# First-block attention scores on 64x64 tiles over 192 queries in every group, and a chunk's raw sums on two column tiles

## The chip, the cores and the metric

The kernel runs on one core of a Trainium2 chip. A core has TensorE (matrix products, PE in the profile, with its weight loads as PEld), VectorE (DVE), ScalarE (ACT), GpSimd (POOL) and SyncE (SP), which here only issues transfers. The engines run side by side, each working through its own queue in order, and wait for each other through semaphores. All share the on-chip memory SBUF; TensorE writes to PSUM, eight banks of 128 partitions with 512 f32 numbers each. Transfers (DMA) run beside the engines, but the instruction that issues one takes time on the queue of the engine that issues it.

The metric is device time in microseconds (us). Before the change the median of three runs is 3545.7 us (3537.46 to 3548.12).

## The reference

The input x is 32 sequences of 256 tokens with 256 channels. A conditioned state-space layer comes first, then two layers of windowed attention and a gated feed-forward, and x is added at the end. Cut to what matters here:

```
xr, gate = split(x @ W_in.T);  xr = xr + cond          # 512 channels each
xc = silu(causal_conv4(xr) + b);  xn = layernorm(xc)
Bm, Cm, dt = split(xn @ W_xproj.T)                     # 16 states each: 48 sums
dt = tanh(dt @ W_dt.T + b_dt) * 0.01
Ad = 1 - dt * tanh(A_log);  Bd = Bm * min(|xn|, 1)
for t:  h = clip(h * Ad[t] + Bd[t] xn[t], -10, 10);  y[t] = Cm[t] . h
cond_out = ((y + D * xn) * silu(gate)) @ W_out.T

for each of 2 layers:
    q, k, v = split(shift(x) @ wqkv)                   # 8 heads of 64
    q, k = rotary(l2norm(q)), rotary(l2norm(k))        # scale 8 on q
    sim[i, j] = q_i . k_j   where  0 <= i - j <= 128,  otherwise masked
    x = x + (softmax(sim) @ v) @ wo
    x = x + (a * gelu(g)) @ w2,   a, g = split(layernorm(shift(x)) @ w1)
out = x_input + x
```

With 256 tokens and windows of 128 there are two blocks of keys. The first block (keys 0 to 127) is seen by all 256 queries, with a mask: key j only by queries j to j + 128. So keys 0 to 63 are seen by queries 0 to 191 at most, and keys 64 to 127 by queries 64 to 255. The second block is seen by queries 128 to 255 only.

## The kernel before

The 32 sequences are four groups of eight (`GB`). For each group the state-space layer is a scan over 256 steps (`group_scan`). It works in chunks of 32 steps (`CH`), so there are eight chunks a group and 32 in all. The states of one step fill 128 partitions (16 states by 8 sequences) with 512 channels; one VectorE instruction (`step`, L722) makes the step. It needs the normalised row of that step, repeated over the states by a transfer (`load_rows`, xrep) and scaled by ScalarE (`scale_row`, L712) two steps ahead. The agenda of the scan is a list of step numbers: `at(s, what)` puts work at step s.

What a chunk needs of figures is made ahead of its first step s0. `raw_sums` (at s0 - 27, L520) multiplies the convolved channels xc of the chunk, 4 blocks of 128 channels by 256 columns (8 sequences by 32 steps), with the 48 columns of W_xproj, widened to 64 with zeros. The sums stand in 64 partitions of a PSUM bank. `raw_copy` (s0 - 25, L528) has ScalarE copy them to SBUF, and `raw_turn` (s0 - 24, L535) issues three transfers on ScalarE's queue, one for each of Bm, Cm and dt, that turn them so that states and sequences lie on 128 partitions and steps on the free axis (`rw`). `figures_in` (s0 - 7, L636) reads rw.

Beside the scan runs the attention and feed-forward of the groups that are done. There are 64 calls of attention (4 groups by 2 layers by 8 sequences), each in eight stages. `scores` (L1232) makes the scores transposed, keys on partitions and queries on the free axis, in parts of one key block and two or four heads with even and odd heads (r = 0, 1) in two PSUM banks, one for each 64 rows of the head dimension. Stage 2 has the first key block of heads 0 to 3 and the whole second block, stage 3 the first block of the others. `exponentials` (L1244) makes exp of both banks.

The mask of the first key block is made in two ways. In group 0 (`apart` is false) a product of an identity and `mask_t` (bf16, L1205) first writes the mask into the whole bank, and the scores are added to it; they come in square pieces of 64 keys by 192 queries, on four quarters of the TensorE array (rows by r, columns by half of the keys). In groups 1 to 3 (`apart`) the scores are written plainly, 128 keys by 256 queries, on two row tiles, and after exp VectorE multiplies by `mask_1`, which is 0 or 1 (L1260). The second block is always one piece of 128 keys by 128 queries on two row tiles, and GpSimd zeroes what is masked (L1255).

All PSUM tiles share the same eight banks (`ps_w`), so TensorE waits when no bank has been freed. The program text is written as one list: scan steps are placed between stages by `scan_to`, and a planner orders the instructions of each engine at compile time, except those that are kept in program order.

Of the kernel before, what the change touches and what calls it, by code (L numbers as in the profile page):

```python
# [10 lines left out]
FP = mybir.dt.float32  # L11
# [8 lines left out]
P = 128  # L20
S = 256
# [3 lines left out]
NC_ = DI // P  # L25
NS = 16
GB = 8
CH = 32
# [9 lines left out]
DH = 64  # L38
W = 128
# [34 lines left out]
def kernel(  # L74
# [29 lines left out]
    nc = tc.nc  # L104
# [58 lines left out]
    for j in range(NJ):  # L163
# [16 lines left out]
    ident_b = const.tile([P, P], BF, tag="ident_b", name="ident_b")  # L180
# [3 lines left out]
        out=mask_t[:, 0:W], in_=mask_t[:, 0:W], compare_op=ALU.is_ge, fill=MASKED_LOW,  # L184
# [3 lines left out]
        out=mask_t[:, W : 2 * W], in_=mask_t[:, W : 2 * W], compare_op=ALU.is_ge,  # L188
# [14 lines left out]
    wx_sb = const.tile([P, NC_, 4 * NS], FP, tag="wx_sb", name="wx_sb")  # L203
# [15 lines left out]
    for i in range(2):  # L219
        t = const.tile([P, NI * (P + GB)], FP, tag=f"ly{i}", name=f"ly{i}")  # L220
# [3 lines left out]
    def program(ctx, exact):  # L224
        rpool = ctx.enter_context(tc.tile_pool(name="res", bufs=1, reuse_waits="tile"))
        wpool = ctx.enter_context(tc.tile_pool(name="weights", bufs=1, reuse_waits="tile"))
        sp = ctx.enter_context(tc.tile_pool(name="sp", bufs=1, reuse_waits="tile"))
# [6 lines left out]
        ps_w = ctx.enter_context(tc.tile_pool(name="psw", bufs=8, space=PSUM, reuse_waits="tile"))  # L234

        def bank(pool, tag, name):
            return pool.tile([P, DI], FP, tag=tag, name=name)
# [141 lines left out]
        def group_scan(g):  # L379
# [12 lines left out]
            ck = [{} for _ in range(NCH)]  # L392
# [122 lines left out]


            def raw_sums(c):
                pr = bank(ps_w, "w", "ps_raw")
                for ch in range(NC_):
                    nc.tensor.matmul(  # L520
                        pr[0 : 4 * NS, 0 : GB * CH], wx_sb[:, ch, :], ck[c]["xc"][:, ch],
                        start=(ch == 0), stop=(ch == NC_ - 1),
                    )
                ck[c]["pr"] = pr

            def raw_copy(c):
                raw = sp.tile([4 * NS, GB * CH], FP, tag="raw", name="raw")
                nc.scalar.copy(raw, ck[c].pop("pr")[0 : 4 * NS, 0 : GB * CH])  # L528
                ck[c]["raw"] = raw

            def raw_turn(c):
                rw = sm.tile([P, 3, CH], FP, tag="rw", name="rw")
                raw = ck[c].pop("raw")
                for i in range(3):
                    nc.scalar.dma_start(  # L535
                        out=rw[:, i],
                        in_=raw[i * NS : (i + 1) * NS].rearrange("n (b t) -> n b t", b=GB),
                    )
                ck[c]["rw"] = rw


# [320 lines left out]
            for c in range(NCH):  # L862
# [14 lines left out]
                for ch, s in enumerate((13, 16, 17, 18)):  # L877
                    at(s0 + s + 2, gate_th, c, ch)
                    if not alone:
                        at(s0 + s + 4, gate_out, c, ch)  # L880
                at(s0 - 25, raw_copy, c)
                at(s0 - 24, raw_turn, c)
                for j in range(NJ):
                    s = s0 - 26 + 4 * j
# [45 lines left out]
            if alone:  # L930
                n = (NG - 1) * NCH * 2
# [130 lines left out]
        if exact:  # L1062
# [4 lines left out]
                out=mask[:, 0:W], in_=mask[:, 0:W], compare_op=ALU.is_ge, fill=MASKED,  # L1067
# [3 lines left out]
                out=mask[:, W : 2 * W], in_=mask[:, W : 2 * W], compare_op=ALU.is_ge, fill=MASKED,  # L1071
# [95 lines left out]
        class Attention:  # L1167
# [51 lines left out]
            def products(self, b, kw, i0, n, banks):  # L1219
                qT, kT, _ = self.qkv[b]  # L1220
                nq = S - kw * W
                masked = kw == 0 and not self.apart
                nm = 2 if masked else 1
                mk = W // nm
                for i in range(n):
                    for r in range(2):
                        rows = slice(r * DH, (r + 1) * DH)
                        for m in range(nm):

                            k0 = m * mk  # L1230
                            q0, q1 = (k0, k0 + W + mk) if masked else (0, nq)
                            nc.tensor.matmul(  # L1232
                                banks[r][k0 : k0 + mk, i, q0:q1],
                                kT[rows, i0 + i, kw * W + k0 : kw * W + k0 + mk],
                                qT[rows, i0 + i, kw * W + q0 : kw * W + q1],
                                start=not masked,
                                stop=not masked or i == n - 1,
                            )
# [328 lines left out]
        for t in range(max(stages) + 1):  # L1567
# [3 lines left out]
            g, r = divmod(t + 1 + group - reload, group)  # L1571
# [124 lines left out]
```

## Time and profile before

| | |
|---|---|
| median of three runs | 3545.7 us |
| the profiled execution | 3535.63 us |
| its span, first to last instruction | 3533.5 us |
| TensorE busy | 3418.2 us |
| ps_raw, L520, 128*64 128x256 f32 | 256 instructions, mean 394 ns |
| rw transfers issued on ScalarE's queue, L535 | 96, median 620 ns |
| sc, L1232, 64*64 64x192 f32 (group 0) | 512 instructions, mean 335 ns |
| sc, L1232, 64*128 64x256 f32 (groups 1 to 3) | 768 instructions, mean 402 ns |
| sc, L1232, 64*128 64x128 f32 (second block) | 1024 instructions, mean 275 ns |

In these rows 64*128 is the part of the array that a product uses (contracted rows by output columns), and 64x256 the moving operand. The mean of one instruction is its latency; products follow each other much closer than that, since they are pipelined, and on different tiles of the array they run side by side. What a run of products costs is therefore read from the timeline, from its first start to the start of what follows. Every f32 product stands as two instructions, one bf16 product as one.

The timeline has start in us, duration in us, engine, line, operation, output and inputs, shape, count, and in brackets the idle time before with what ended it. The stretches have for each engine its busy time and its number of instructions, then granted clock, share of the DMA engines, and GB/s. ACTq is the queue of ScalarE, where transfers are issued. A group row has its busy time and the mean of one instruction.

### The profile page before, as it was taken

Reading aid. Unit: us, or ns where it says so; the run is one execution under the profiler, and the core shown is the slowest. Engines: PE = TensorE matmul, PEld = TensorE weight load, DVE = VectorE, ACT = ScalarE, POOL = GpSimd, SP = SyncE. Lnnn points to the kernel's source line nnn. Section 1 sums busy time; section 2 is a strip of 40 time slices with the busy share of each in tenths; the row PEclk is TensorE's granted clock in tenths of the full one; section 3 lists DMA queues with packets and bytes.
Section 4 is the critical chain, followed back from the end, with each engine's and each line's share of the span. In section 5 each row is a group of like instructions: output and inputs, shape, how many; then the busy total and the mean of one; then the engine's idle time right before and its main releaser. Section 6 shows DMA issues by size and latency. Waiting matters only on the chain.

```text
span 3533.5 us, 56484 instructions
## 1 busy us (share of the span) xinstructions
PE 3418.2 (97%) x19580; PEld 2257.4 (64%) x19580; DVE 2683.2 (76%) x5177; ACT 2035.4 (58%) x3663; POOL 1625.6 (46%) x1587
## 2 busy tenths in 40 slices
PE   7999989999999999999999999999999999999999
PEld 4545335666666666666666666666666777777777
DVE  5888898878788788888888888888787655555563
ACT  4666656656666665666666656666566444444442
POOL 4433456544455555544455555544444434333441
PEclk9999999999999999999999999999999999999999
DMA  7787655545454555444454555544444212011111
GB/s 208 215 217 218 198 169 153 136 113 142 129 143 130 150 147 151 136 114 134 117 142 128 148 148 147 137 120 130 118 142 118 61 37 62 13 31 36 37 28 38
DMA packets 487195, 436.65 MB, mean 124 GB/s; under 512 B 247155, under 2 KB 326516, under 8 KB 486772
## 3 DMA queue, kind: packets, MB, share of 16 engines
q1 hardware_dynamic: 401426, 420.41, 42.2%
q10 hardware_dynamic: 85474, 12.53, 2.1%
q8 instruction: 157, 2.57, 0.3%
q14 instruction: 138, 1.13, 0.1%
HBM read 384.06 MB, written 47.19 MB: 122 GB/s over the span
## 4 chain that ended last, share of the span: by engine, by line
PE 63%; DVE 17%; DMA 7%; POOL 5%; ACT 4%; issue 3%; SPq 1%; ACTq 0%; DVEq 0%; POOLq 0%
PE ps_qkv L996 13%; PE pa L1405 13%; DVE h L722 7%; PE po_f L1432 6%; PE y L734 5%; PE ps_wo L1052 4%; PE ov L1289 3%; DMA xrep<-xnd 3%; PE ps_out L814 3%; PE ps_in L401 3%; PE sc L1232 3%; PE tr_qk L1041 2%; PE rs L1269 2%; PE ps_raw L520 2%; DVE acc L491 1%
## 5 line engine op out<-in xcount | busy, mean ns | idle before, releaser
L722 DVE CUSTOM_DVE_ANT_0 h<-h,xrep,lim 128x512 f32<-128x512 f32 x1024 | 917.2, 896 | 137.3 <-ACT xrep L712 93.4
L712 ACT ACTIVATE xrep<-xrep,beta 128x512 f32<-128x512 f32 x960 | 671.6, 719 | 265.5 <-DMA xrep<-xnd 178.2
L996 PE MATMUL ps_qkv<-qkv,res 128*128 128x512 f32 x1536 | 716.0, 601 | 26.6 <-DVE ag L1423 12.5
L1405 PE MATMUL pa<-hT,w 128*128 128x256 f32 (+1 forms) x2816 | 674.7, 382 | 5.1 <-DVE zT L805 5.1
L1405 PEld LDWEIGHTS pa<-hT,w 128*128 128x128 f32 (+1 forms) x2816 | 517.4, 188 | 145.4 <-issue 41.8
L1020 POOL TENSOR_TENSOR rot<-rot,swp 128x512 f32<-128x512 f32 x256 | 345.1, 1348 | 496.7 <-DVE swp L1017 465.9
L996 PEld LDWEIGHTS ps_qkv<-qkv,res 128*128 128x128 f32 x1536 | 282.0, 191 | 311.5 <-issue 247.0
L1026 POOL TENSOR_TENSOR rn<-ss,neg_half 128x8 f32<-128x8 f32 x256 | 457.6, 1788 | 0.0
L734 PE MATMUL y<-h,ly 128*32 128x512 f32 x2048 | 341.1, 606 | 15.7 <-DVE h L722 13.6
L1432 PE MATMUL po_f<-ag,w 128*128 128x256 f32 x1280 | 306.7, 387 | 3.8 <-DVE fo L1443 3.1
L1423 DVE SCALAR_TENSOR_TENSOR ag<-pa,b_sb,ag 128x256 f32<-128x256 f32 x320 | 151.5, 474 | 208.7 <-ACT ag L1416 208.7
L1009 ACT ACTIVATE sq<-ps_qkv,tiny 128x512 f32<-128x512 f32 x256 | 173.3, 685 | 186.3 <-PE ps_qkv L996 129.3
L1432 PEld LDWEIGHTS po_f<-ag,w 128*128 128x128 f32 x1280 | 235.3, 190 | 68.3 <-DVE pT L1260 12.9
L1416 ACT ACTIVATE ag<-pa,b_sb 128x256 f32<-128x256 f32 x320 | 150.0, 469 | 209.7 <-PE pa L1405 206.8
L1357 POOL TENSOR_TENSOR rstd<-ve,neg_half 128x2 f32<-128x2 f32 x64 | 46.5, 726 | 484.9 <-DVE ve L1355 484.8
L1052 PE MATMUL ps_wo<-oT,wo 128*128 128x256 f32 x1024 | 231.6, 379 | 0.0
L1012 DVE TENSOR_TENSOR rot<-ps_qkv,rc_sb 128x512 f32<-128x512 f32 x256 | 175.1, 684 | 71.8 <-ACT sq L1009 70.1
L491 DVE SCALAR_TENSOR_TENSOR acc<-xr,wc_sb,acc 128x256 f32<-128x256 f32 x384 | 183.1, 499 | 50.8 <-POOL acc L480 50.0
L1017 DVE TENSOR_TENSOR swp<-ps_qkv,rs_sb 128x256 f32<-128x256 f32 x512 | 191.8, 416 | 27.6 <-POOL rot L1020 27.5
L1052 PEld LDWEIGHTS ps_wo<-oT,wo 128*128 128x128 f32 x1024 | 194.5, 190 | 27.2 <-ACT th_g L774 0.8
L1032 DVE SCALAR_TENSOR_TENSOR rot<-rn,rot 128x512 f32<-128x512 f32 x256 | 205.7, 841 | 7.5 <-POOL rn L1026 7.5
L1244 ACT ACTIVATE pT<-sc 128x512 f32<-128x512 f32 x384 | 201.6, 601 | 8.2 <-PE sc L1232 6.1
(161 smaller groups left out, 5375.6 us busy)
## 6 DMA issues: line engine op xcount, KB each, us to landing
xrep<-xnd SPq DMA_DIRECT2D x960, 256.0 KB
rb<-inv SPq DMA_DIRECT2D x128, 256.0 KB
xnd<-xn SPq DMA_DIRECT2D x64, 256.0 KB
qkv<-in_wqkv_dram SPq DMA_DIRECT2D x24, 512.0 KB
ahead<-xs_a SPq DMA_DIRECT2D x48, 256.0 KB
xp<-ahead SPq DMA_DIRECT2D x48, 256.0 KB
xd<-xnd SPq DMA_DIRECT2D x192, 64.0 KB
w<-in_w_dram SPq DMA_DIRECT2D x80, 128.0 KB
```

The source lines that it names most:

```text
L491: nc.vector.scalar_tensor_tensor(acc, xr[:, :, k : k + CH], wc_sb[:, ch, k : k + 1], acc, ALU.mult, ALU.add,)
L712: scaled = nc.scalar.activation(bx, ck[c].pop(("bx", t), bx), AF.Copy, scale=ck[c]["beta"][:, t : t + 1])
L722: nc.vector._custom_dve(TENSOR_ADD_SAT, out=h_new, in0=state["h"], in1=bx, s0=ck[c]["lim"][:, 0, t : t + 1], s1=ck[c]["lim"][:, 1, t : t + 1],
L734: nc.tensor.matmul(ck[c]["y", hb][32 * q : 32 * q + 32, :], ly[hb % 2][:, 32 * t : 32 * t + 32], ck[c].pop(("h", hb * TB + t)), start=(i = ...
L996: nc.tensor.matmul(ps, res[b][:, k, t0 : t0 + W], wt["qkv", a][:, k], start=(k == 0), stop=(k == KM - 1),)
L1020: nc.gpsimd.tensor_add(rot, rot, swp)
L1026: nc.gpsimd.tensor_tensor(rn, ss, neg_half, ALU.pow)
L1032: nc.vector.scalar_tensor_tensor(rot, bc(rn, 2, DH), 1e12, rot, ALU.min, ALU.mult)
L1052: nc.tensor.matmul(po[:, d], wt["wo", 0][:, c, d * P : (d + 1) * P], oT[:, c, :], start=(c == 0), stop=(c == NC_ - 1),)
L1244: nc.scalar.activation(p, banks[r], AF.Exp)
L1405: nc.tensor.matmul(dst[x], wt["w1", m][:, k, x], self.h[:, k], start=(k == 0), stop=(k == KM - 1),)
L1432: nc.tensor.matmul(self.po[:, d], wt["w2", 0][:, m, d * P : (d + 1) * P], self.ag[m], start=(m == 0), stop=(m == len(MCH) - 1),)
```

## The change

Raw sums: each of the four products of a chunk becomes two, for the first and the last 16 steps of all sequences, on column tiles 0 to 63 and 64 to 127 of the array. They write to partitions 0 to 63 and 64 to 127 of the same 128 columns of a bank. ScalarE's copy is then 128 partitions by 128, and six transfers of half the size bring it to the same `rw`.

Scores: every part is made in square pieces of 64 keys. In the first key block the pieces span 192 queries in all groups. In groups 1 to 3, where nothing is written beforehand, the 64 queries that a piece leaves out get zeros from one bf16 product for each tile of the array and part (an identity's off-diagonal block, which is zero, times columns of the identity), for all heads of the part at once. Their exp is 1, and the multiplication by `mask_1` makes them 0 as before. The second key block is two pieces of 64 keys by 128 queries.

```diff
--- before.py
+++ after.py
@@ -515,27 +515,34 @@
 
 
             def raw_sums(c):
-                pr = bank(ps_w, "w", "ps_raw")
+                pr = bank(ps_w, "w", "ps_raw")[:, 0 : GB * CH // 2]
+                halves = ck[c]["xc"].rearrange("p c (b h t) -> p c b h t", b=GB, h=2)
                 for ch in range(NC_):
-                    nc.tensor.matmul(
-                        pr[0 : 4 * NS, 0 : GB * CH], wx_sb[:, ch, :], ck[c]["xc"][:, ch],
-                        start=(ch == 0), stop=(ch == NC_ - 1),
-                    )
+                    for h in range(2):
+                        nc.tensor.matmul(
+                            pr[64 * h : 64 * h + 64],
+                            wx_sb[:, ch, :],
+                            halves[:, ch, :, h],
+                            start=(ch == 0),
+                            stop=(ch == NC_ - 1),
+                        )
                 ck[c]["pr"] = pr
 
             def raw_copy(c):
-                raw = sp.tile([4 * NS, GB * CH], FP, tag="raw", name="raw")
-                nc.scalar.copy(raw, ck[c].pop("pr")[0 : 4 * NS, 0 : GB * CH])
+                raw = sp.tile([P, GB * CH // 2], FP, tag="raw", name="raw")
+                nc.scalar.copy(raw, ck[c].pop("pr"))
                 ck[c]["raw"] = raw
 
             def raw_turn(c):
                 rw = sm.tile([P, 3, CH], FP, tag="rw", name="rw")
                 raw = ck[c].pop("raw")
-                for i in range(3):
-                    nc.scalar.dma_start(
-                        out=rw[:, i],
-                        in_=raw[i * NS : (i + 1) * NS].rearrange("n (b t) -> n b t", b=GB),
-                    )
+                for h in range(2):
+                    for i in range(3):
+                        r = 64 * h + i * NS
+                        nc.scalar.dma_start(
+                            out=rw[:, i, h * CH // 2 : (h + 1) * CH // 2],
+                            in_=raw[r : r + NS].rearrange("n (b t) -> n b t", b=GB),
+                        )
                 ck[c]["rw"] = rw
 
 
@@ -1220,15 +1227,23 @@
                 qT, kT, _ = self.qkv[b]
                 nq = S - kw * W
                 masked = kw == 0 and not self.apart
-                nm = 2 if masked else 1
-                mk = W // nm
+                mk = W // 2
                 for i in range(n):
                     for r in range(2):
                         rows = slice(r * DH, (r + 1) * DH)
-                        for m in range(nm):
+                        for m in range(2):
 
                             k0 = m * mk
-                            q0, q1 = (k0, k0 + W + mk) if masked else (0, nq)
+                            if kw == 0 and not masked and i == 0:
+                                qc = (S - mk) * (1 - m)
+                                nc.tensor.matmul(
+                                    banks[r][k0 : k0 + mk, :, qc : qc + mk],
+                                    ident_b[rows, (1 - r) * DH : (2 - r) * DH],
+                                    ident_b[rows, 0 : n * mk],
+                                    start=True,
+                                    stop=True,
+                                )
+                            q0, q1 = (0, nq) if kw else (k0, k0 + W + mk)
                             nc.tensor.matmul(
                                 banks[r][k0 : k0 + mk, i, q0:q1],
                                 kT[rows, i0 + i, kw * W + k0 : kw * W + k0 + mk],
```

## The prediction

> **What bounds the kernel now.** I read the page's busy shares first, then the chain, then the stretches.
>
> ```profile
> span 3533.5 us, 56484 instructions
> PE 3418.2 (97%) x19580; PEld 2257.4 (64%) x19580; DVE 2683.2 (76%) x5177; ACT 2035.4 (58%) x3663; POOL 1625.6 (46%) x1587
> PE 63%; DVE 17%; DMA 7%; POOL 5%; ACT 4%; issue 3%; SPq 1%; ACTq 0%; DVEq 0%; POOLq 0%
> ```
> ```profile
> core 0: us, PE busy (x) PEld busy (x) DVE busy (x) ACT busy (x) POOL busy (x), PEclk, DMA share, GB/s
> 0.00:500.00 500.00, 445.62 (x1847) 230.16 (x1848) 411.83 (x758) 296.18 (x545) 211.36 (x306) 0.95 0.76 209
> 500.00:2600.00 2100.00, 2047.03 (x12277) 1357.03 (x12276) 1734.90 (x3397) 1313.15 (x2389) 1072.68 (x1012) 1.00 0.49 135
> 2600.00:3400.00 800.00, 800.00 (x4717) 571.01 (x4716) 480.53 (x907) 382.96 (x654) 310.49 (x245) 1.00 0.20 54
> ```
>
> TensorE is the bound. From 500 to 2600 us, where the recurrent scan runs beside attention, it is idle 53 of 2100 us, 2.5%. After 2600 us it is never idle. Only before 500 us (TensorE 89%) does VectorE's chain of steps set a good part of the pace. A busy share can hide slack, so the parts are costed by starts: from the first instruction of a run to the start of the next one on TensorE.
>
> ```profile
> 503.19 0.59 PE L1205 MATMUL sc<-mask_t,ident_b 128*128 128x512 bf16 x2
> 503.71 1.97 PE L1232 MATMUL sc<-qT,kT 64*64 64x192 f32 x32
> 505.62 1.06 PE L734 MATMUL y<-h,ly 128*32 128x512 f32 x6
> ...
> 507.14 0.88 PE L1232 MATMUL sc<-qT,kT 64*64 64x192 f32 x16
> 507.95 2.41 PE L996 MATMUL ps_qkv<-qkv,res 128*128 128x512 f32 x5
> ```
> ```profile
> 2018.32 2.02 PE L1232 MATMUL sc<-qT,kT 64*128 64x256 f32 x24
> 2020.27 2.42 PE L1432 MATMUL po_f<-ag,w 128*128 128x256 f32 x10
> ...
> 2023.50 1.13 PE L1232 MATMUL sc<-qT,kT 64*128 64x256 f32 x8
> 2024.56 1.98 PE L996 MATMUL ps_qkv<-qkv,res 128*128 128x512 f32 x4
> ```
> ```profile
> 2051.31 1.52 PE L1289 MATMUL ov<-pT,v_sb 128*64 128x256 f32 x16 [0.28 <-DVE ag L1423]
> 2052.76 0.64 PE L734 MATMUL y<-h,ly 128*32 128x512 f32 x4
> ```
> ```profile
> 2477.26 1.94 PE L520 MATMUL ps_raw<-xc,wx_sb 128*64 128x256 f32 x8
> 2479.13 0.66 PE L550 MATMUL tp_x<-ident,xc 128*128 128x128 f32 x4
> ...
> 2479.63 1.93 ACTq L535 DMA_DIRECT2D rw<-raw  x3
> ...
> 2481.67 0.72 ACT L712 ACTIVATE xrep<-xrep,beta 128x512 f32<-128x512 f32 x1 [1.44 <-DVE h L722]
> 2485.09 0.29 ACT L574 ACTIVATE stat<-nm,stat 128x1 f32<-128x1 f32 x1 [2.70 <-POOL stat L567]
> ```
>
> An f32 product is two instructions in these rows (two passes). The first two fences are the same work in two forms: group 0 (four square tiles, 192 queries) and a later group (two row tiles, 256 queries). A first-block part of two heads takes 507.95 - 507.14 = 0.81 us in the square form and 2024.56 - 2023.50 = 1.06 in the other. With the second key block behind it, the run takes 505.62 - 503.71 = 1.91 and 2020.27 - 2018.32 = 1.95.
>
> **Raw sums, TensorE.** Now eight passes of 256 columns follow each other: 2479.13 - 2477.26 = 1.87 us, that is 8 x 0.216 and 0.14 of entry and exit. (The chain gives 3.43 us for eight passes of 512 columns at L996: 0.43 each, 0.84 ns a column, 0.216 for 256.) Afterwards there are sixteen passes of 128 columns on two column tiles. The values line already runs in that form: its sixteen passes are four pairs of 256 columns and four of 128 and take 2052.76 - 2051.31 = 1.45; less 4 x 0.216 and 0.14 this leaves 0.45, or 0.11 for a pair of 128. So 8 x 0.109 + 0.14 = 1.01, and 0.86 us less for each of 32 chunks. The moving operand becomes runs of 16 elements at a stride of 32; no matmul of the trace shows such a pattern, so the gain lies between 0 (the stride costs what the split saves) and 0.86. I take 0.86: the nearest row, the mask product at L1205 whose moving operand is a repeated pattern and not one run, takes 0.26 us for 512 bf16 columns and shows no penalty. 22 chunks lie after 500 us: 18.9 us. Ten lie in the stage that TensorE only half bounds: half of 8.6, 4.3 us. Together 23.
>
> The values row shows that the two column tiles load their weights beside running products. [...]
>
> **Raw sums, ScalarE and transfers.** The copy goes from 64x256 (363 ns) to 128x128. A 128x32 activation takes 318, so it saves 0 to 0.05 us; I take 0.03. The three issues of rw become six, at a median of 620 ns (552 to 1394) each on ScalarE's queue: 1.86 us more a chunk, net 1.83 x 32 = 58.6 us of ScalarE's time. Queued behind them are the scaling of the scan's rows (L712), which VectorE's step (L722) waits for, then L574 and L581, and copies that free PSUM banks for TensorE. The last fence shows the cover: after the burst ScalarE scales one row and then sits 2.70 us until GpSimd has delivered. 1.83 fits, and rows are scaled two steps ahead of use. In early chunks the idle time comes later. Bounds 0 and 58.6 us; I take 5, near the lower end, because of that gap. The transfers move the same bytes in 64-byte runs; figures_in, which reads them, is due 17 steps after the issue, at least 17 x 0.9 = 15 us (a step, L722, takes 896 ns), against 3.7 us of issuing. SP's and GpSimd's queues are not touched.
>
> **First key block, groups 1 to 3 (48 calls, 96 parts).** 1.06 becomes 0.81 plus the four zero fills of a part (64x128, bf16). Two mask products take 503.71 - 503.19 = 0.52 us: 0.26 for 512 columns, 0.065 for 128. If the four tiles fill side by side the price is 0.065; hidden under other loads it is 0; one after another it is 0.26, the whole gain; worse is a rival below. I take 0.065, since everything else on the four tiles runs side by side. Gain 0.25 - 0.065 = 0.185, x 96 = 17.8 us.
>
> **Second key block, all 64 calls.** Now 1.95 - 1.06 = 0.89 for eight steps of 0.111, set by loading 128 weight columns (187 ns each in the groups by shape, against 132 for 64). Square tiles stream 128 columns in 0.109 and load half as many: 0.02 x 64 = 1.3 us less, though twice the instructions. The bounds are that and no gain, as issue is cheap: group 0 starts four tiles within 0.02 us. In group 0 the change of tiling between the blocks goes too: 1.91 becomes 0.81 + 0.87 = 1.68, of which 0.02 is counted, so 0.21 x 16 = 3.4 us. VectorE's mask product and the exponentials keep shape and count.
>
> **Sum.** TensorE loses 23.2 + 17.8 + 1.3 + 3.4 = 46 us. Of the 64 calls, 22 lie after 2600 us: 22 x 0.39 = 9 us, kept whole. 37 lie before. Of these 37 I keep 0.8, as TensorE there waits 2.5% of the time for banks that VectorE (83% busy) frees, and reaches those waits sooner: 30. Less 5 on ScalarE: 34 us. The profiled execution took 3535.6 us (span 3533.5), so 3502 on its scale; that execution lies 10 us under the median of 3545.7, against which the forecast is 3511.
>
> **Rivals.**
> *Six issues in a burst (slower).* If ScalarE's 1.83 us a chunk reached the end whole, 58.6 against a kept 39 (9 + 30): +20, 3565. It decides from 39 / 58.6 = two thirds of each burst, 1.2 us. For it: after the issues at 791 us ScalarE runs on without a gap until 801. Against: the 2.70 us gap.
> *The fills break the overlap (slower).* In each tile the fill and two f32 passes now stand in a row. If the next tile's fill waits for this tile's first pass, three tiles start 0.065 + 0.162 us later each (0.162 is a 192-column pass at 0.84 ns a column): 0.68 x 96 = 65 us, so 34 gained becomes 31 lost: 3577. Against: the square run in group 0 shows sixteen passes in the time of four. [...]
> *Gains given back.* If VectorE's and ScalarE's chains set the pace up to 2600 us, only the 9 us of the tail stay, less 5: 3542, no change. For it: 17% of the chain is VectorE. Against: TensorE's 97.5% there.
> *The order shifts.* The order on each engine is planned at compile time, and other durations may change who goes first; the present waits for PSUM banks (53 us from 500 to 2600) could double: -34 + 53 = +19, 3565.
>
> **Chances.** Forecast 0.62 (its own range 3489 to 3533), gains given back 0.15, six issues 0.10, fills 0.07, order 0.06. A measurement of this kernel tells about 0.3% (10.6 us) from nothing. Faster: 0.60 and 0.04; the same: 0.02, 0.10 and 0.02; slower: the rest, 0.22. The range reaches from 3489 (nothing lost, 3500, less the 11 us by which the three runs differ) to 3566, past the end of two of the slower cases.
>
> **What would show it.** Right: raw-sum runs near 1.0 us with 512 passes of 128*64 128x128; lone first-block parts near 0.88 and joined runs near 1.75; no 64*128 form left; TensorE's busy time near 3372. A strided operand that costs would show as ps_raw runs above 1.1; broken overlap as lone parts above 1.3. Six issues that hurt show as a wait of L722 for L712 well above 93 us. The prediction is wrong if TensorE's idle time between 500 and 2600 us grows by more than 30 us while its runs shrink as told.

## The result, and the profile after

| | before | after |
|---|---|---|
| median | 3538.69 us (10 runs, 3534.73 to 3548.12) | 3551.04 us (10 runs, 3539.09 to 3555.05) |
| ratio after / before | | 1.0027, 95% interval 1.0016 to 1.0039 |
| span of the profiled execution | 3533.5 us | 3552.0 us |

The changed kernel is no faster. It is about 10 us slower by the ratio (12 by the medians), where 34 us less were forecast: inside the 0.3% that were called no change, but on the wrong side of it.

The page of the kernel after: its span, the busy shares, and the chain of work that ended last.

```profile
span 3552.0 us, 61405 instructions
PE 3398.7 (96%) x22012; PEld 2240.8 (63%) x22012; DVE 2675.2 (75%) x5177; ACT 2021.0 (57%) x3663; POOL 1606.0 (45%) x1587
PE 62%; DVE 17%; DMA 9%; POOL 4%; ACT 4%; issue 3%; SPq 1%; ACTq 0%; DVEq 0%; POOLq 0%
```

Its stretches, in the columns of the table of before.

```profile
core 0: us, PE busy (x) PEld busy (x) DVE busy (x) ACT busy (x) POOL busy (x), PEclk, DMA share, GB/s
0.00:500.00 500.00, 438.32 (x1859) 223.88 (x1860) 380.22 (x721) 281.56 (x527) 193.30 (x294) 0.93 0.76 203
500.00:2600.00 2100.00, 2018.64 (x13677) 1335.04 (x13679) 1743.35 (x3392) 1302.52 (x2384) 1046.34 (x1010) 0.99 0.50 135
2600.00:3400.00 800.00, 798.70 (x5535) 570.87 (x5527) 483.68 (x930) 383.55 (x660) 324.89 (x252) 1.00 0.22 58
```

TensorE's busy time did fall, but its idle time grew instead of the end coming sooner: from 500 to 2600 us it is idle 81 us, where it was 53. In the first 500 us VectorE does 32 us less work than before (380.22 where it was 411.83): the scan is late there.

On TensorE itself the runs came out as forecast. The timeline of the kernel after, TensorE alone (start, duration, engine, line, operation, tiles, shape, count):

```profile
530.26 1.75 PE L1247 MATMUL sc<-qT,kT 64*64 64x192 f32 x48
531.94 1.06 PE L741 MATMUL y<-h,ly 128*32 128x512 f32 x6
...
1999.12 1.09 PE L522 MATMUL ps_raw<-xc,wx_sb 128*64 128x128 f32 x16
2000.15 0.66 PE L557 MATMUL tp_x<-ident,xc 128*128 128x128 f32 x4
...
2043.02 0.27 PE L1239 MATMUL sc<-ident_b 64*64 64x128 bf16 x4
2043.10 1.72 PE L1247 MATMUL sc<-qT,kT 64*64 64x192 f32 x48
2044.75 2.43 PE L1447 MATMUL po_f<-ag,w 128*128 128x256 f32 x10
...
2047.97 0.27 PE L1239 MATMUL sc<-ident_b 64*64 64x128 bf16 x4
2048.05 0.84 PE L1247 MATMUL sc<-qT,kT 64*64 64x192 f32 x16
2048.82 1.98 PE L1003 MATMUL ps_qkv<-qkv,res 128*128 128x512 f32 x4
```

From start to next start, the raw sums take 2000.15 - 1999.12 = 1.03 us (before 1.87, forecast 1.01), the lone first-block part with its fills 0.85 (before 1.06, forecast 0.88), and the part joined with the second block 1.73 (before 1.95, forecast 1.75). In group 0 the joined run takes 531.94 - 530.26 = 1.68 (before 1.91, forecast 1.68). The strided operand costs nothing that shows (1.03 against 1.01), the fills do not break the overlap (0.85 with them, 0.81 for the square form of group 0 without), and the column tiles load their weights beside running products: the sixteen loads of this raw-sum run, 137 ns each by the median, stand within its first 0.85 us. Busy time in all was a miss, though: 3398.7 us, 20 less than before, where 3372 had been named. Of the 26 us between, 15 are time at half clock, which takes 49 us of full clock in the trace of after (mean granted clock 0.986 over 3552.0 us) and 34 in that of before (0.990 over 3533.5).

**Where the time is lost.** The traces give the start of the first scan step, of attention calls 0 and 40 (the first ov product of each) and the end. This table has how much later than before each comes; the three columns behind are the differences: the first stage (to call 0, 525.0 us in before), the middle (call 0 to call 40, which starts at 2551.7 us in before) and the tail.

| | first stage | middle | tail | end of span |
|---|---|---|---|---|
| forecast (us, of the 34) | +5 - 4 | -24 | -10 | -34 |
| after | +26.2 | +1.3 | -9.0 | +18.5 |

The forecast's row splits its own sum, to 1 us: the kept 30 us are 0.8 of 37, of which some 30 lie in the middle (20 chunks of raw sums, 17.2; 24 calls of groups 1 to 3 by 0.39; 16 calls of group 0 by 0.23) and 5 in the first stage (half of the first ten chunks, and the eleventh). The last chunk and two of the 42 calls that the prediction places before 2600 us run behind call 40. Issues were costed at 5, with no stage named; they stand in the first here.

The tail is right within 1 us. The middle gains nothing, and the first stage loses. These are two questions. One caution holds for all milestones: a profile is one execution, and its first stage swings by some 10 us from the median of the same kernel, so beside the profiled first stage stands the estimate "median's difference less middle and tail". For the change it is 0.0027 x 3538.7 - 1.3 + 9.0 = 17 us. In part the swing stands ahead of the scan's first step, which comes 5.4 us later than before in the trace of after, 7.2 later in e4 and 1.8 in e5 (whose first stages have the same edit), and 11.6 later in k1 (these runs are told below).

### The profile page after: what moved, and what is told of

Read it like the earlier page. It is cut to its first block, busy times and chain, and to the rows that moved or that the text cites. A ratio compares the mean times of both kernels' runs of the same rounds, so it can differ in the third digit from the quotient of the medians.

```text
span 3552.0 us, 61405 instructions
## 1 busy us (share of the span) xinstructions
PE 3398.7 (96%) x22012; PEld 2240.8 (63%) x22012; DVE 2675.2 (75%) x5177; ACT 2021.0 (57%) x3663; POOL 1606.0 (45%) x1587
## 4 chain that ended last, share of the span: by engine, by line
PE 62%; DVE 17%; DMA 9%; POOL 4%; ACT 4%; issue 3%; SPq 1%; ACTq 0%; DVEq 0%; POOLq 0%
PE ps_qkv L1003 13%; PE pa L1420 12%; DVE h L729 7%; PE po_f L1447 7%; DMA xrep<-xnd 5%; PE y L741 5%; PE ps_wo L1059 4%; PE ov L1304 4%; PE ps_in L401 3%; PE ps_out L821 3%; PE sc L1247 2%; PE tr_qk L1048 2%; PE rs L1284 2%; PE ps_a L428 1%; ACT xrep L719 1%
## 5 line engine op out<-in xcount | busy, mean ns | idle before, releaser
L1003 PE MATMUL ps_qkv<-qkv,res 128*128 128x512 f32 x1536 | 716.7, 603 | 40.9 <-DVE xd L792 13.8
L741 PE MATMUL y<-h,ly 128*32 128x512 f32 x2048 | 358.3, 612 | 15.3 <-DVE h L729 14.8
L491 DVE SCALAR_TENSOR_TENSOR acc<-xr,wc_sb,acc 128x256 f32<-128x256 f32 x384 | 192.9, 522 | 51.9 <-POOL acc L480 50.3
L1039 DVE SCALAR_TENSOR_TENSOR rot<-rn,rot 128x512 f32<-128x512 f32 x256 | 193.1, 792 | 6.7 <-POOL rn L1033 6.7
```

The costliest lines, as they stand in the source:

```text
L491: nc.vector.scalar_tensor_tensor(acc, xr[:, :, k : k + CH], wc_sb[:, ch, k : k + 1], acc, ALU.mult, ALU.add,)
L741: nc.tensor.matmul(ck[c]["y", hb][32 * q : 32 * q + 32, :], ly[hb % 2][:, 32 * t : 32 * t + 32], ck[c].pop(("h", hb * TB + t)), start=(i = ...
L1003: nc.tensor.matmul(ps, res[b][:, k, t0 : t0 + W], wt["qkv", a][:, k], start=(k == 0), stop=(k == KM - 1),)
L1039: nc.vector.scalar_tensor_tensor(rot, bc(rn, 2, DH), 1e12, rot, ALU.min, ALU.mult)
```

## The experiments

Each line is against the kernel before on the same chip, with a 95% interval. The first stage is as profiled, and in brackets by the estimate above.

| run | ratio | first stage | middle | tail |
|---|---|---|---|---|
| after | 1.0027 [1.0016, 1.0039] | +26 (17) | +1.3 | -9.0 |
| e1: raw sums alone, six issues | 1.0044 [1.0030, 1.0059] | +15 (21) | -6.1 | +0.3 |
| e2: scores alone | 0.9994 [0.9982, 1.0007] | -3 (3) | +4.5 | -9.8 |
| e3: six issues alone | 1.0055 [1.0042, 1.0068] | +21 (15) | +3.5 | +0.8 |
| e4: raw sums alone, three issues | 1.0011 [1.0002, 1.0020] | +20 (22) | -16.8 | -1.1 |
| e5: both, three issues | 1.0002 [0.9994, 1.0011] | +17 (24) | -12.5 | -10.6 |
| k1: six issues in group 0 alone | 1.0024 [1.0012, 1.0035] | +19 (9) | -0.9 | +0.6 |
| x1: two copies alone | 0.9997 [0.9987, 1.0007] | +2 (3) | -4.2 | +0.1 |
| n5: another order alone | 1.0001 [0.9990, 1.0012] | 0 (0) | +0.2 | 0.0 |
| h1: after, group 0's raw sums as before | 0.9986 [0.9977, 0.9995] | +8 (6) | -3.0 | -7.8 |
| h2: h1 with three issues | 0.9945 [0.9932, 0.9959] | +3 (4) | -13.5 | -10.0 |
| p1: before, no mask product | 0.9948 [0.9933, 0.9963] | -1 (5) | -22.4 | -1.4 |
| p2: e5, no mask product | 0.9971 [0.9961, 0.9982] | +21 (13) | -12.6 | -10.9 |
| t0: before, oT on VectorE | 0.9982 [0.9973, 0.9992] | -3 (-2) | -1.9 | -2.2 |
| t1: h2, oT on VectorE | 0.9919 [0.9906, 0.9933] | +4 (6) | -22.4 | -12.0 |
| t2: after, oT on VectorE | 0.9981 [0.9971, 0.9992] | +18 (25) | -21.0 | -10.6 |
| s0: before, no mask product, oT on VectorE | 0.9958 [0.9944, 0.9972] | -2 (3) | -17.7 | -0.5 |
| s2: h2, no mask product, oT on VectorE | 0.9853 [0.9840, 0.9866] | -1 (3) | -43.7 | -11.1 |

### The parts one by one

e1 has only the column tiles, the one copy and the six issues of the diff. e2 has only the scores. e3 keeps TensorE as it was and cuts the transfers:

```diff
-                for i in range(3):
-                    nc.scalar.dma_start(
-                        out=rw[:, i],
-                        in_=raw[i * NS : (i + 1) * NS].rearrange("n (b t) -> n b t", b=GB),
+                for h in range(2):
+                    ts = slice(h * CH // 2, (h + 1) * CH // 2)
+                    for i in range(3):
+                        nc.scalar.dma_start(
+                            out=rw[:, i, ts],
+                            in_=raw[i * NS : (i + 1) * NS].rearrange("n (b t) -> n b t", b=GB)[:, :, ts],
```

e5 has both parts of the change on TensorE, but two copies put the halves side by side again, and the three issues of before follow:

```diff
             def raw_copy(c):
                 raw = sp.tile([4 * NS, GB * CH], FP, tag="raw", name="raw")
+                halves = raw.rearrange("p (b h t) -> p h b t", b=GB, h=2)
+                pr = ck[c].pop("pr").rearrange("p (b t) -> p b t", b=GB)
+                for h in range(2):
+                    nc.scalar.copy(halves[:, h], pr[64 * h : 64 * h + 64])
```

> Raw sums on two column tiles with their six issues; the scores stay as before. Theory A (the six issues on ScalarE's queue cost more than the column tiles save): the scan of group 0 is as late as in the changed kernel, +25 us at its 256th step, the stretch up to 2600 us gives nothing back, and the total is +20 to +35 us (about 3565). Theory B (the loss comes from the order that the planner chose for all edits together, the issues themselves are covered): +-10 us, with the 256th step less than 10 us late.

> Square tiles in all groups with zero fills; the raw sums stay as before. Theory A: nothing of the first stage moves, the 64 calls gain what TensorE's runs gain, 0.2 to 0.4 us each: -15 to -25 us (about 3518). Theory B: the new order costs what the runs gain, 0 to +15 us. In both, the tail after 2600 us gains 0.4 us a call, 9 us.

> Nothing on TensorE changes: the raw sums stay as before, but each of the three transfers is cut into two of half the steps, so six issues on ScalarE's queue. This measures the disputed cost by itself, at most 32 x 1.86 = 60 us. Theory A: +40 to +60 us (about 3590), the 256th step 25 us late and the rest spread over the chunks up to 2600 us. Theory B: 0 to +10 us, since ScalarE has idle time behind the burst.

> Both edits on TensorE, but ScalarE copies the two halves side by side into the old 64x256 layout (two copies of about 0.25 us in place of one of 0.36), so that three issues are enough. Theory A: the first stage is no later than before and TensorE's gain is mostly kept, -30 to -45 us (about 3503). Theory B: no better than the changed kernel, 3540 to 3560.

Six issues alone cost 0.55%, 19 us, all but some 4 us of it before call 0. That lies between the two theories for e3, and e1's 16 us between the two for e1: the issues are neither covered nor paid in full. The scores alone gain the tail's 10 us and lose 4.5 in the middle, where 0.8 of 13 had been forecast as a gain. And e5 shows that the issues are not all: with three of them the first stage still loses, and neither of its theories came true. Its 0.0002 is a gain of 23 us behind call 0 that the stage ahead of it has eaten.

### Is it only another order?

An edit of a duration can make the planner order all engines anew. n5 changes the order and nothing else. It has the same instructions, with the raw sums' agenda one and two steps later.

```diff
-                at(s0 - 25, raw_copy, c)
-                at(s0 - 24, raw_turn, c)
+                at(s0 - 24, raw_copy, c)
+                at(s0 - 22, raw_turn, c)
...
-                at(s0 - 27, raw_sums, c)
+                at(s0 - 26, raw_sums, c)
```

> The kernel before with not one instruction changed in kind or number: raw_sums and raw_copy are put one step later and raw_turn two, so that the planner finds another order (VectorE's and ScalarE's order differs most). If the order alone can cost what the first stage of the other kernels lost: the 256th step or the total moves by 5 to 15 us. If the order hardly matters: within 4 us.

It does nothing. So this other order is no loss of itself. It is a mild one, though: by the names of the tiles some 60 of ScalarE's 3663 instructions stand elsewhere than in before, some 270 in after. Which instruction is put ahead of which must be found.

### The middle: a copy behind a waiting scaling

What TensorE waited for between 1650 and 2350 us, in the view of waits (us in all, times, longest), in before:

```profile
PE ps_qkv L996 <- DVE ag L1423: 6.0, 6, 1.6
PE ps_qkv L996 <- DVE xd L785: 4.8, 7, 0.7
PE sc L1232 <- DVE swp L1017: 2.7, 7, 1.0
```

and after:

```profile
PE ps_qkv L1003 <- ACT oT L1311: 7.6, 7, 1.3
PE ps_qkv L1003 <- DVE xd L792: 6.9, 7, 1.0
PE sc L1239 <- DVE swp L1024: 6.3, 7, 0.9
```

All are waits for a PSUM bank that another engine must empty: none of the tiles named behind the arrow is an operand of the product that waits. VectorE's have grown a little, as TensorE comes to them sooner. One is new, the largest: ScalarE's copy oT, which no wait of before names in these 700 us. The timeline of ScalarE and TensorE after shows why it is late.

```profile
1977.62 0.59 ACT L1311 COPY oT<-ov 128x512 f32<-128x512 f32 x1 [0.69 <-PE pa L1420]
...
1981.48 0.72 ACT L719 ACTIVATE xrep<-xrep,beta 128x512 f32<-128x512 f32 x1 [3.27 <-DMA xrep<-xnd]
1982.10 0.57 ACT L1311 COPY oT<-ov 128x512 f32<-128x512 f32 x1
...
1982.72 3.27 PE L1003 MATMUL ps_qkv<-qkv,res 128*128 128x512 f32 x7 [1.33 <-ACT oT L1311]
```

The same place in before:

```profile
1954.06 1.07 ACT L1296 COPY oT<-ov 128x512 f32<-128x512 f32 x2 [0.69 <-PE pa L1405]
1955.02 0.73 ACT L712 ACTIVATE xrep<-xrep,beta 128x512 f32<-128x512 f32 x1
```

Before, both copies go first. After, a row scaling that waits 3.27 us for its transfer stands between the two, and the second copy, whose operand has been there since 1974.6 us (the end of the ov products), waits behind it. TensorE loses 1.33 us for the bank.

Two rivals had to be told apart: VectorE, which is 83% busy and holds the other banks, and this copy. p1 and p2 leave out VectorE's mask product in groups 1 to 3 (145 us of its work), so that the masked scores stay in, in the kernel before and in e5.

```diff
-                        masked = nc.vector.tensor_mul(p, p, bc(mask_1[:, 0:nq], 1, n))
+                        continue
```

> The kernel before without VectorE's mask product of the first key block in groups 1 to 3 (192 products of 0.75 us, 145 us of VectorE; the masked scores stay in, so the output differs). If VectorE, through the PSUM banks it frees, sets the pace between 500 and 2600 us: -25 us or more. If TensorE alone sets it: within 8 us of the kernel before.

> The kernel with both edits on TensorE and three issues, without that mask product (same part left out). If VectorE is what takes TensorE's gain back, the gain shows once VectorE is relieved: 20 to 40 us below the run of the kernel before without the mask. If something else takes it: no more than the 9 us of the tail below that run.

Before gains 22.4 us in the middle by it. This is what TensorE waits for in p1 in the same 700 us:

```profile
PE ps_qkv L996 <- DVE xd L785: 4.6, 7, 0.7
PE ov L1289 <- DVE ag L1423: 2.0, 4, 0.5
PE sc L1232 <- DVE swp L1017: 0.2, 1, 0.2
```

The 6.0 us for ag at L996 are gone, and most of swp's. In before, no product of TensorE waits for the masked scores themselves. So not TensorE alone but VectorE's releases set its pace; some 5 of the 22.4 us are TensorE's clock, which that one execution had at half for a shorter time (in before, half clock takes 6.8 us of the middle). The total, 18 us less, is short of the 25 of its theory. e5 gains nothing there (-12.6 where it had -12.5), where 20 to 40 us were expected had VectorE alone taken the gain. So after the change other releases held TensorE too. t0, t1 and t2 keep the mask and move the copy:

```diff
-                    nc.scalar.copy(oT[:, i0 : i0 + 2], ov)
+                    nc.vector.tensor_copy(oT[:, i0 : i0 + 2], ov)
```

> The kernel before with the copies of oT out of PSUM made by VectorE in place of ScalarE, nothing else. Before, TensorE's waits name VectorE (ag, xd, zT, swp) and not oT, so more work on VectorE can only lengthen them: 3537 to 3560 against 3536, the loss between 525 and 2600 us.

> Square scores everywhere, column tiles with two copies and three issues in groups 1 to 3 (0.9945 as it is), and oT copied by VectorE. If ScalarE's place for oT is what holds the rest of TensorE's gain back, this run is another 8 to 15 us faster: 3500 to 3507 against 3536. If VectorE with the mask product has no room, as the waits for ag, xd and swp say, it is equal to or slower than the variant without: 3512 to 3535.

> The changed kernel with oT copied by VectorE. Its trace has TensorE wait most for ScalarE's oT (7.6 of 30 us from 1650 to 2350). If ScalarE's queue of six issues and oT is the cause: 10 to 20 us less than the changed kernel, 3528 to 3538 against 3536. If the bank waits go to VectorE: 3545 to 3565.

In the changed kernel this one line turns +1.3 us in the middle into -21.0; in before it is worth 1.9. Over the whole middle, TensorE's waits for oT add up to 13.2 us in after; a further 3.4 us are less time at half clock, and the rest is in no wait that the view names. The waits of t2 in the same 700 us no longer name oT, and VectorE's have not grown, though it has more to do:

```profile
PE ps_qkv L1003 <- DVE xd L792: 6.9, 7, 1.0
PE sc L1239 <- DVE swp L1024: 6.3, 7, 0.9
PE pa L1420 <- DVE zT L812: 3.2, 4, 0.8
```

I had expected of t0 a loss or nothing. That VectorE had room for these copies was a miss.

s0 and s2 take both away, the mask product and ScalarE's oT, in the kernel before and in h2.

> The kernel before without VectorE's mask product in groups 1 to 3 (that part is left out), and with the copies of oT out of PSUM (two for each pair of heads) made by VectorE in place of ScalarE. It is the partner of the next run. Without the mask alone the kernel took 0.9948 with TensorE 99% busy, so moving oT can bring little more: 3510 to 3522 against 3537.

> Square scores everywhere, column tiles with two copies and three issues in groups 1 to 3, the mask product left out and oT copied by VectorE, as in the run before. If the waits that ate TensorE's gain are those for ScalarE's copies of oT (which stand behind a row scaling in the new order) and for a loaded VectorE, the gain shows here: 0.9 us less of TensorE a call from 500 to 2600 us (about 30 us) and 9 in the tail, 25 to 40 us less than the run before. If they move to the next release whatever is relieved, the difference is 0 to 12 us, mostly in the tail, and TensorE's idle time from 500 to 2600 us stays 20 us or more above that run's.

TensorE from 500 to 2600 us in s0:

```profile
500.00:2600.00 2100.00, 2063.98 (x12422) 1370.97 (x12421) 1749.72 (x3403) 1285.89 (x2333) 1077.51 (x1016) 1.00 0.50 137
```

and in s2:

```profile
500.00:2600.00 2100.00, 2057.64 (x14076) 1378.35 (x14075) 1775.66 (x3447) 1304.24 (x2385) 1090.34 (x1027) 1.00 0.50 139
```

Now the new forms leave TensorE idle 42 us where the old ones leave it 36, and the new forms (with three issues) take -43.7 + 17.7 = -26.0 us off the middle: a little more than the 24 that the forecast had kept for it. With ScalarE's copy and the mask in place the same edits had returned between +1.3 and -13.5. The saving on TensorE was real all along; it was the waits that ate it.

### The six issues, and the group where they hurt

h1 is the changed kernel with the raw sums of group 0 as before. h2 is h1 with e5's two copies and three issues.

```diff
+            if alone:
+                def raw_sums(c):
+                    pr = bank(ps_w, "w", "ps_raw")
...
+            else:
+                def raw_sums(c):
+                    pr = bank(ps_w, "w", "ps_raw")[:, 0 : GB * CH // 2]
...
```

> The changed kernel, but group 0 keeps the old raw sums (one column tile, three issues); groups 1 to 3 have column tiles and six issues, and the scores are on square tiles. Theory C (the loss lies in the first stage, where ScalarE's six issues and the order around them hold up the scan; later the issues are covered): the 256th step is less than 5 us late and the total is -5 to -15 us (about 3524). Theory D (six issues cost in every chunk): still +5 to +15 us, lost after the 256th step.

> Square scores everywhere and column tiles for the raw sums in groups 1 to 3 alone, there with two copies and three issues; group 0 keeps the old raw sums, copy and issues. TensorE's work falls by about 0.4 us a call for the scores and 0.86 us a chunk. If bank releases by the other engines set the pace from 500 to 2600 us, only the tail's 9 us come, less what the order costs: 3528 to 3534 against 3537, near the variant of it with six issues (0.9986). If the six issues of the later groups had held that one back: 3515 or less.

Group 0's old form brings the first stage back to +3 to +8 us. And the issues cost in the later groups too: 10.7 us of the middle between e1 and e4 (-6.1 and -16.8), and 10.5 between h1 and h2, where about 5 us of the pair's difference are time at half clock (11.9 and 6.8 us lost by it in the middle; e1 and e4 5.1 and 6.8). Here h2's expectation failed: it gave 0.9945, where I thought it would stand beside h1. With oT off ScalarE the issues cost almost nothing in the middle: t2, with six, gains -21.0 there, t1, with three, -22.4. So here too it is what stands in ScalarE's queue behind them that counts. t1 is the fastest version that computes all that the reference does, 0.9919 [0.9906, 0.9933].

k1 cuts the transfers into six in group 0 alone.

> The kernel before with the three transfers of rw cut into six only in group 0 (the first eight chunks, up to about 525 us); sums, copies and scores as before. If the cost of six issues lies in the first stage, as the milestones of the run with six issues everywhere say (21 us of its loss by the first attention call), this run loses nearly the same: +17 to +22 us, 3554 to 3559 against 3537, and the loss stands at the first attention call and doesn't grow. If the loss there only happened to be a difference of order, it may be within 5 us of before.

Its median is 8 us up and its middle even. Its profile shows +19, but that one execution took 3554.49 us, 11.5 more than the median of k1, and 11.6 of the 19 us are there before the scan's first step. So group 0's six issues cost about 9 of the 15 to 21 us that e3 loses in the first stage; the first chunks of group 1, whose sums also run before call 0, may be the rest, which was not tried.

### The first stage: who waits behind whom

What VectorE's step waited for between 48 and 460 us, in before (and the two waits of ScalarE that matter below):

```profile
DVE h L722 <- ACT xrep L712: 12.9, 16, 3.4
ACT sq_x L594 <- POOL xn L589: 9.6, 9, 3.1
ACT xrep L712 <- DMA rw<-raw: 1.5, 1, 1.5
```

after:

```profile
DVE h L729 <- ACT xrep L719: 29.9, 29, 4.3
ACT xrep L719 <- DMA rw<-raw: 21.7, 7, 5.9
```

and one chunk of it in the timeline of after:

```profile
65.19 6.40 ACTq L542 DMA_DIRECT2D rw<-raw  x6
71.64 0.72 ACT L719 ACTIVATE xrep<-xrep,beta 128x512 f32<-128x512 f32 x1 [5.89 <-DMA rw<-raw]
...
72.40 0.81 DVE L729 CUSTOM_DVE_ANT_0 h<-h,xrep,lim 128x512 f32<-128x512 f32 x1 [2.74 <-ACT xrep L719]
```

The six issues span 6.40 us here. One takes 1.81 us and the others 0.55 to 0.74, with a gap of 1.3 us in between. The row scaling stands behind them, and the step behind that. Rows are scaled two steps ahead; a step takes 0.8 to 0.9 us. Over the stage the scaling waits 21.7 us behind such bursts, where it waited 1.5.

But e4 and e5 have three issues and lose as much. e4 is e5 without the new scores, x1 is before with the second copy alone:

```diff
-                nc.scalar.copy(raw, ck[c].pop("pr")[0 : 4 * NS, 0 : GB * CH])
+                pr, k = ck[c].pop("pr"), GB * CH // 2
+                for h in range(2): nc.scalar.copy(raw[:, h * k : h * k + k], pr[0 : 4 * NS, h * k : h * k + k])
```

> The kernel before with the column tiles for the raw sums in all groups, two copies and three issues; scores as before. If the column tiles or the second copy lose in the first stage by themselves: +12 to +20 us at the first attention call, and a total of 3545 to 3556 against 3536. If only six issues or the pair with the new scores lose there: within 5 us at the first call, total 3525 to 3536.

> The kernel before with ScalarE's copy of the raw sums in two halves of 64 partitions by 128, in all groups; the sums on TensorE and the three issues as before. The second copy is 32 x about 0.3 us of ScalarE's time. If the loss in the first stage comes from one more instruction on ScalarE there, or from the order that this brings: +12 to +20 us by the first attention call, 3543 to 3555 against 3533. If it comes from the column tiles on TensorE: within 5 us at the first call, total 3528 to 3540.

The second copy is not it; the loss comes with the column tiles. It does not come from their time, which falls. The total of e4 fell outside the range expected (3545 to 3556), as the middle gave back 16.8 us. In e4 steps 79, 110, 143, 175 and 206 (counted from 0), one in each of five chunks, wait 1.4 to 3.0 us; in before these steps wait 0.3 at most. The waits of e4 from 48 to 460 us:

```profile
DVE h L722 <- ACT xrep L712: 30.0, 24, 7.0
ACT sq_x L594 <- POOL xn L589: 17.8, 8, 2.9
```

and the timeline of e4 at step 110:

```profile
227.95 0.61 ACT L825 ACTIVATE yo<-ps_out 128x256 f32<-128x256 f32 x1 [1.93 <-PE ps_out L814]
228.37 0.73 ACT L581 ACTIVATE xn<-tp_x,stat 128x512 f32<-128x512 f32 x1
...
232.17 0.63 ACT L594 ACTIVATE sq_x<-xn 128x512 bf16<-128x512 f32 x1 [2.42 <-POOL xn L589]
232.80 1.32 ACT L712 ACTIVATE xrep<-xrep,beta 128x512 f32<-128x512 f32 x2
...
233.54 0.81 DVE L722 CUSTOM_DVE_ANT_0 h<-h,xrep,lim 128x512 f32<-128x512 f32 x1 [2.54 <-ACT xrep L712]
```

where before has, a chunk earlier:

```profile
164.27 0.78 ACT L581 ACTIVATE xn<-tp_x,stat 128x512 f32<-128x512 f32 x1
166.00 0.63 ACT L825 ACTIVATE yo<-ps_out 128x256 f32<-128x256 f32 x1 [0.95 <-PE ps_out L814]
...
168.19 0.61 ACT L594 ACTIVATE sq_x<-xn 128x512 bf16<-128x512 f32 x1
```

Before, the normalisation xn goes ahead of yo; GpSimd has finished with it by the time that its squares sq_x are due (in other chunks of before sq_x waits for it too, up to 1.5 us, and 3.1 once). In e4 yo goes first and waits 1.93 us for TensorE, xn comes after it though it was ready, GpSimd is late by that, sq_x waits 2.42 us for GpSimd, and the row scaling that VectorE needs stands behind sq_x. This is read off the trace. That the swap of yo and xn alone makes the loss was not tried, and why the planner makes it with the column tiles stays open.

It can't be the whole loss. Step by step, e4 is 7.2 us later than before at step 0, 13.8 at step 64, 16.3 at step 192 and 20.9 at step 255. Four of the five waits lie between steps 64 and 192 and add up to 9 us, but only 2.5 us of it stay. The rest arises ahead of them and behind. In after the same four steps are 5.4, 8.6, 11.3 and 20.2 us late. Nor do the parts add up here: by the estimates, six issues alone lose 15 us in the first stage (e3), column tiles alone 22 (e4), both together 21 (e1).

A rival stands untested: TensorE's granted clock. Its mean over the span is 0.991 to 0.992 in the runs of before beside the experiments and 0.991 in p1, s0 and s2, but 0.9855 in the ten runs of after and 0.9865 in e5 and t2. Among executions of one kernel, 0.001 less goes with about 2 us more (an estimate, one slope through all runs on record), so 0.006 would go with 12 us, as much as the change loses. By the traces half clock takes 37.5 us of full clock (half of its duration) before call 0 in after and 25.6 in before, but only 10.2 and 6.8 in the middle. The granted clock is lowest where TensorE is idle most: in after 0.93 in the first 500 us, with 62 us of them idle, 0.99 from 500 to 2600 us, with 81 of 2100 idle, and 1.00 from 2600 to 3400 us, with 1 of 800. So it may be an effect of the late scan as much as a cause; no run parts the two.

## Why the prediction was wrong, step by step

- **Raw sums, first block, second block and group 0 on TensorE: right.** 1.87 to 1.03, 1.06 to 0.85, 1.95 to 1.73, 1.91 to 1.68 us, each within 0.03 of the forecast. The doubt that the fills break the overlap fell (0.85 us, where a broken overlap was to show above 1.3), and so did the one about the stride (1.03 us, where its cost was to show above 1.1).
- **The tail, kept whole: right**, 9.0 for some 10 (e2 9.8). TensorE is all but never idle there (in after 1.3 of 800 us from 2600 to 3400).
- **"Of these 37 I keep 0.8": the step that failed.** The middle kept none of some 30, where 24 were to be kept. The reason given, idle time of 2.5%, was no measure of slack, and it named VectorE's releases alone. p1 shows what it hid: with VectorE relieved, the old kernel's middle is 22 us shorter with the same products, so bank releases were setting part of the pace already. With both releasers relieved (s0 to s2) 26 us come out. As it is, the new order put a waiting row scaling between two copies of oT, and t2 shows that with these copies off ScalarE the middle is 22 us shorter.
- **"Less 5 on ScalarE": the second step that failed, mis-sized by a factor of about four.** The 2.70 us gap that was to cover a burst is in a late chunk (2482 us). In the first stage the row scaling waits behind the bursts instead (21.7 us in after, 1.5 in before). An issue costs there what it was taken for (0.55 to 0.74 us in the burst shown, for a median of 0.62), with few exceptions (1.81 once in that burst); what was missed is what stands behind it. e3 measured 19 us for six issues (0.0055 x 3534), some 15 to 21 of them in the first stage; e1 against e4 and h1 against h2 show another 11 in the middle once TensorE is faster.
- **"Half of 8.6" in the first stage: wrong in sign.** Column tiles lose about 20 us there even with three issues (e4), and hardly any once group 0 keeps the old form (h2, 3 to 4). Why they lose is shown only in part. No step of the prediction looked at what stands beside what in ScalarE's queue after the planner has seen shorter sums.
- **The rivals.** "Gains given back" (3542, tail kept, middle lost) has the shape of the result behind call 0; the loss of the first stage comes on top of it. The mark set for being wrong, over 30 us more idle time from 500 to 2600, was all but met: 28.

Behind call 0 the parts add up. In the middle, e4's -16.8 and e2's +4.5 make -12.3 (e5 -12.5, h2 -13.5), and 11 for six issues make about -2 (after +1.3). With 17 to 26 us lost in the first stage and 9 won in the tail this is the 10 to 18 us by which the change is slower: 25 us of the miss lie in the middle and 16 or more in the first stage.

## What to carry to other kernels

An engine that is 97% busy is not thereby the bound: before a saving on it is booked, ask which releases it waits for, and take those engines' work away in a trial. If the end moves, as it did in p1 (22.4 us in the middle), the saving will be kept only in part. What six issues in place of three cost on ScalarE's queue went by what stood behind them: 10.7 us of the middle with oT on that queue (e1 against e4), 1.4 with oT off it (t2 against t1), 15 to 21 us in the first stage (e3). So look at each stage's own queue, the first one above all, and not at a gap found elsewhere. And where a planner orders the program, an edit of one engine's durations can put a waiting instruction ahead of a ready one on another; look in the trace after for a ready copy behind a wait.

## What was not expected of the hardware

TensorE's granted clock fell in h1 right behind two waits of less than 1 us. They take 0.90 and 0.98 us and come within 2.8 us, and the four product instructions behind them, which take 1.98 us in h2, take 3.62. The stretches and the timeline of h1:

```profile
1975.50:1980.00 4.50, 4.00 (x8) 1.34 (x12) 4.22 (x7) 0.96 (x3) 4.50 (x4) 0.62 0.95 232
```
```profile
1974.08 0.27 PE L1252 MATMUL sc<-ident_b 64*64 64x128 bf16 x4 [0.90 <-DVE swp L1039]
...
1975.99 3.62 PE L1018 MATMUL ps_qkv<-qkv,res 128*128 128x512 f32 x4 [0.98 <-DVE xd L807]
```

and of h2, with the same two waits:

```profile
1961.23 0.28 PE L1253 MATMUL sc<-ident_b 64*64 64x128 bf16 x4 [0.90 <-DVE swp L1040]
...
1963.14 1.98 PE L1019 MATMUL ps_qkv<-qkv,res 128*128 128x512 f32 x4 [0.98 <-DVE xd L808]
```

The granted clock is 0.62 over the stretch in h1. In h2 waits of the same length leave the four instructions at 1.98 us. So the fall cost 3.62 - 1.98 = 1.64 us in the one, and there was none in the other; what decides it was not shown. Such time is small in the middle here: half clock there takes 6.8 us of full clock in before and 10.2 in after.
